# First run over bands: when its statistics, reciprocal roots and biases are issued

## The chip, the cores and the metric

The kernel runs on one core of a Trainium2 chip. The metric is device microseconds of one execution. Engines are called as in the profile: PE (matrix multiply, with PEld for its weight loads), DVE (vector), ACT (scalar functions), POOL (GpSimd) and SP, whose queue issues the transfers. Each engine runs its instructions in the order of its queue.

## The reference

The input x has shape 2 x 256 x 128 x 128 (batch, time, band, channel), float32. Three residual blocks follow one another, each on a layer norm over the 128 channels:

```python
xt = _ln(x, ln_t_w, ln_t_b).transpose(0, 2, 1, 3)
x = x + _mha(xt, t_wi, t_bi, t_wo, t_bo, H_T, cm).transpose(0, 2, 1, 3)
xf = _ln(x, ln_f_w, ln_f_b)
x = x + _mha(xf, f_wi, f_bi, f_wo, f_bo, H_F, bm)
xn = _ln(x, ln_n_w, ln_n_b)
h = jax.nn.gelu(xn @ w1.T + b1, approximate=False)
x = x + (h @ w2.T + b2)
```

The first attention runs over time (256 positions, causal), the second over bands (128 positions, at most 16 apart), both with four heads of 32 channels. The layer norm needs, for each position, the mean, the variance and 1/sqrt(variance + 1e-5).

## The kernel before

**Groups.** The work is cut into 384 groups of 512 positions (four tiles of 128 x 128). Groups 0 to 127 are `OverTime`: the attention over time, whose result goes to a DRAM buffer. After them come 16 runs. Each run has 8 `OverBands` groups and then 8 `FeedForward` groups over the same positions; the result of the bands stays on chip in tiles called x2 (shown as x in the profile). The first run is groups 128 to 135 (bands) and 136 to 143 (feed-forward).

**Steps.** One loop in `BoundedPath.run` goes over n. In step n the engines work on several groups at once: scores and exponentials of group n, the weighing with values and the row sums of group n-1 (`weigh`), their inversion and the division of n-1 (`invert`, `divide`), the output product and residual sum of n-2 (`output`, `finish`), and, for groups ahead, statistics, normalization, a turn through DRAM, and the products for queries, keys and values. Every instruction is pinned to program order (`InOrder`), so the order in which the loop calls these methods is the order of each engine's queue; nothing is moved by the scheduler. PSUM has eight banks that are handed round in turn, or by a fixed table in the time steps; a bank's next use waits for the engine that still reads it.

**Normalizing one group.** `statistics` issues four bn_stats and four bn_aggr on DVE (tiles stats and mv). The root comes in two ways. `root` is done by POOL alone: an addition of epsilon and a power, into rstd. `root_by_scalar` is done by ACT with Ln and Exp (lnv, root), and `refine` follows on DVE with three scalar_tensor_tensor instructions on 128 x 4 elements (vy, vy, rstd). `normalize` issues four tensor_scalar on DVE (xh), `turn` a transpose on DVE (z) and four transfers. Time groups use the second way in step n-5 (statistics and refinement of group n+5 in step n), band and feed-forward groups the first, except those of the first run.

**Biases.** `bias` is one tensor_tensor on POOL per group: x plus a row, into the tile that the group's output is later added to by `finish`. A time step has two masks over 128 x 1024 and two additions on POOL besides the time group's bias; a band step has six masks over 128 x 512 (three of the four heads, two sides). The fourth head's mask is added on DVE (sp<-sp,band). In a feed-forward step of one run POOL also does the bias and the root of the next run's bands.

**The first run.** It has no run before it, so its preparation falls into the last time steps. With A = 8, step n of 120 to 127 issues, after the division, the statistics of group n+8 on DVE and its bias on POOL; step n+1 issues `root_by_scalar` and `refine` of that group. So group 128 has its statistics in step 120 and its refinement in step 121, and group 135 in steps 127 and 128. `normalize` of a band group is in the third step before its own, `finish` in the second after it. Time statistics end with step 122, time normalization with step 123.

Of the kernel before, what the change touches and what calls it, by code (L numbers as in the profile page):

```python
# [25 lines left out]
NT = 4  # L26
GA = 8
GB = 16
RUN = 32
# [698 lines left out]
def time_scores(old, new):  # L728


    if new is not None:
        new.first_tiles()
    if old is not None:
        old.second_tiles()
    for h, second, s in (
        (0, 1, 0), (1, 0, 0), (2, 0, 0), (3, 1, 0), (0, 1, 1), (3, 1, 1), (0, 0, 0), (3, 0, 0),
        (1, 0, 1), (2, 0, 1), (0, 0, 1), (3, 0, 1), (1, 1, 0), (2, 1, 0), (1, 1, 1), (2, 1, 1),
    ):
        if second and old is not None:
            old.second_scores(h, s)  # L740
        if not second and new is not None:
            new.first_scores(h, s)
# [123 lines left out]
class BoundedPath:  # L866
# [164 lines left out]
    def run(self, x, out):  # L1031
        groups = list(self.groups(x, out))

        def do(n, *names):
            if 0 <= n < len(groups):
                for name in names:
                    getattr(groups[n], name)()

        def at(n, kind):
            return 0 <= n < len(groups) and isinstance(groups[n], kind)  # L1040

        def do_at(n, kind, *names):
            if at(n, kind):
                do(n, *names)

        A = RUN // NT

        self.scalar.preload_act_table_set(EXP_SET)
        for n in range(-12, len(groups) + 2):
            feeds = [at(n - 2 + i, FeedForward) for i in range(5)]  # L1050
            bands = [at(n - 2 + i, OverBands) for i in range(5)]
            turn = feeds[2] and bands[1]
            old, new = (groups[i] if at(i, OverTime) else None for i in (n, n + 1))
            self.by_columns = at(n - 1, Attention)
            if bands[2] and feeds[1]:
                self.scalar.preload_act_table_set(EXP_SET)
            do_at(n + 4, FeedForward, "root")
            do(n, "first_half", "first_function", "first_mask")
            if old is not None or new is not None:
                time_scores(old, new)  # L1060
                b = self.banks
                Attention.place = dict(rp=b["b0"], op=b["b3"], yp=b["a1"], qp=b["a2"], kp=b["b1"], vp=b["b2"])
            else:
                Attention.place = {}
            if old is not None:
                old.second_weights(old.late)
            if new is not None:
                new.first_weights(new.early)
            if old is not None:
                old.second_weights(old.early)  # L1070
                old.mask_second()
                old.add(0)
            if turn:
                do(n, "second_half", "second_function")
            do_at(n + 3, OverTime, "fetch")
            do_at(n + 2, (OverBands, FeedForward), "fetch")

            for i in (2 * n + 12, 2 * n + 13) if n < -2 else (n + 10,) if n < 2 else ():
                if i >= NT:
                    do(i, "load")  # L1080
            if n < -8 or n >= 0:
                do(n + 12, "load")
            if n >= 0:
                do_at(n + 5, OverTime, "statistics")
            do_at(n + 3, (OverBands, FeedForward), "normalize", "turn")
            do_at(n + 4, OverTime, "normalize", "turn")
            if n < 0:
                do(n + 5, "statistics")
            do_at(n + 5, FeedForward, "statistics")
            if n == -4:  # L1090
                self.fold_rest()
                self.warm()
            do(n - 1, "weigh")
            do(n - 1, "invert_exactly" if turn else "invert")
            if new is not None:
                new.first_weights(new.late)
                new.mask_first()
            if old is not None:
                old.add(1)
            if bands[2] or turn or old is not None:  # L1100
                do(n - 2, "output", "finish")
            do(n - 1, "divide")
            if not turn:
                do(n, "second_half", "second_function")
            if not bands[2]:
                do_at(n, FeedForward, "bias")
                do_at(n + A, OverBands, "bias")
                if at(n - 1, FeedForward) and at(n - 2, OverBands):
                    do_at(n + A - 1, OverBands, "statistics", "root")
                if not turn:  # L1110
                    do_at(n + A, OverBands, "statistics")
                    if not at(n, OverTime):
                        do_at(n + A, OverBands, "root")
            do_at(n + 2, OverTime, "queries_keys", "take_query", "take_key")
            do_at(n + 1, OverBands, "queries_keys", "take_query", "take_key")
            do_at(n + 5, OverTime, "root_by_scalar", "refine")
            if at(n - 1, OverTime):
                do_at(n + A - 1, OverBands, "root_by_scalar", "refine")
            do_at(n, OverTime, "bias")
            if not bands[2] and not turn and old is None:  # L1120
                do(n - 2, "output", "finish")
            do_at(n + 2, OverTime, "values", "take_values")
            do_at(n + 1, OverBands, "values", "take_values")
            if old is not None or new is not None:

                b = self.banks
                self.banks = dict(
                    a1=b["a1"], a2=b["a2"], b0=b["a0"], b3=b["a3"], a0=b["b0"], a3=b["b1"], b1=b["b3"], b2=b["b2"]
                )
# [69 lines left out]
```

## Time and profile before

| | us |
|---|---|
| median of 4 runs (2729.62 to 2731.49) | 2730.57 |
| the profiled execution's own time | 2729.83 |
| its span in the profile | 2728.1 |
| PE busy | 2698.6 |
| DVE busy | 2282.0 |
| POOL busy | 1864.4 |
| ACT busy | 1847.5 |

The span is the time from the first to the last instruction that the profile holds; the execution's own time has some 1.7 us around it. Busy is the sum of an engine's instructions. A row of the timeline gives start, duration, engine, operation, out<-in, and in brackets the idle time before it and what ended it. In a row of stretches each engine has its busy time and number of instructions, and then come the granted clock of PE (1.00 is full), the share of the DMA engines and what they moved. All instructions issued through the helper have line 861, so they are told apart by their tiles. The time groups end at about 979 us of the span, the first run's band steps at about 1032.

### The profile page before, as it was taken

The page shows a single profiled execution, that of the slowest core. Times are in us where ns is not written, and L with a number is a line of the kernel's source. Part 1 is how long each engine was busy: PE and PEld are TensorE (multiplying, and loading weights), DVE is VectorE, ACT ScalarE, POOL GpSimd, SP SyncE. Part 2 cuts the span into 40 slices and gives each one's busy share as a digit, 9 for nine tenths or more (in the row PEclk, how much of TensorE's full clock was granted, in tenths as well). Part 3 has the DMA queues.
Part 4 walks back from the last instruction along what each step waited for, and adds up shares of the span by engine and source line. Part 5 has one row for each costly group of instructions (what it writes and reads, how often), then busy time and mean ns, then how long its engine had stood idle before and what let it go on. Part 6 is the DMA issues. An engine that isn't in the chain of part 4 may idle for free.

```text
span 2728.1 us, 105787 instructions
## 1 busy us (share of the span) xinstructions
PE 2698.6 (99%) x43538; PEld 1885.2 (69%) x43538; DVE 2282.0 (84%) x6708; ACT 1847.5 (68%) x3620; POOL 1864.4 (68%) x2169
## 2 busy tenths in 40 slices
PE   8999999999999999999999999999999999999998
PEld 5666767767767667676676676766766767767666
DVE  7999999999999997968869779688697796886874
ACT  6888888888888874655745646556556465465563
POOL 3887888888788876666657666666576666665762
PEclk9999999999999999999999999999999999999999
DMA  5555555555555544445444444454453444544533
GB/s 147 145 149 142 146 152 141 148 150 143 143 154 144 135 105 123 114 117 125 112 119 124 108 120 118 117 127 109 120 127 105 120 119 113 133 106 117 133 91 79
DMA packets 471309, 343.83 MB, mean 126 GB/s; under 512 B 43296, under 2 KB 405152, under 8 KB 470816
## 3 DMA queue, kind: packets, MB, share of 16 engines
q1 hardware_dynamic: 469568, 335.92, 48.1%
q8 instruction: 344, 5.64, 0.9%
q14 instruction: 149, 1.22, 0.2%
q10 hardware_dynamic: 1248, 1.05, 0.2%
HBM read 169.03 MB, written 167.77 MB: 123 GB/s over the span
## 4 chain that ended last, share of the span: by engine, by line
PE 73%; DVE 20%; DMA 3%; issue 2%; SPq 1%; POOL 0%; ACT 0%; DVEq 0%; ACTq 0%
PE zp L861 17%; PE hp L861 14%; PE sp L861 8%; PE op L861 6%; PE rp L861 6%; PE vp L861 5%; PE qp L861 5%; PE kp L861 5%; PE yp L861 5%; DVE xh L861 4%; DVE stats L861 3%; DVE u L861 2%; DVE z L861 2%; DVE rp L861 2%; DMA xnT<-turned 2%
## 5 line engine op out<-in xcount | busy, mean ns | idle before, releaser
L861 ACT ACTIVATE hT<-hp,b 128x512 f32<-128x512 f32 x512 | 348.0, 687 | 543.5 <-PE hp L861 532.6
L861 POOL TENSOR_SCALAR_AFFINE_SELECT pf<-pf 128x512 f32<-128x512 f32 x768 | 478.7, 638 | 273.0 <-ACT pf L861 246.8
L861 DVE TENSOR_SCALAR xh<-x,mv,rstd 128x160 f32<-128x160 f32 x1536 | 597.1, 431 | 14.2
L861 PEld LDWEIGHTS zp<-w2T_sb,hT 128*128 128x128 f32 x4096 | 476.3, 192 | 56.2 <-issue 54.1
L861 PE MATMUL zp<-w2T_sb,hT 128*128 128x128 f32 x4096 | 479.8, 275 | 0.1
L861 PE MATMUL hp<-xnT,w1f 128*128 128x512 f32 x1024 | 469.2, 596 | 0.0
L861 ACT ACTIVATE p<-sp 128x512 f32<-128x512 f32 (+1 forms) x1024 | 417.5, 499 | 18.8 <-PE sp L861 6.5
L861 POOL TENSOR_SCALAR_AFFINE_SELECT p<-p 128x1024 f32<-128x1024 f32 x256 | 281.0, 1097 | 185.7 <-ACT p L861 185.6
L861 PE MATMUL sp<-qT,kT 32*128 32x128 f32 (+1 forms) x8192 | 362.9, 310 | 4.7 <-DVE oT L861 2.2
L861 PEld LDWEIGHTS sp<-qT,kT 32*128 32x128 f32 x8192 | 310.6, 185 | 56.0 <-ACT kT L861 44.4
L861 PEld LDWEIGHTS vp<-wf,xnT 128*32 128x32 f32 (+1 forms) x7400 | 237.4, 113 | 153.3 <-issue 137.0
L861 POOL TENSOR_TENSOR p<-p,p 128x512 f32<-128x512 f32 x256 | 329.0, 1285 | 10.7
L861 DVE BATCH_NORM_STATS2 stats<-x 128x6 f32<-128x128 f32 x1536 | 327.0, 275 | 0.1
L861 ACT ACTIVATE pf<-sp 128x512 f32<-128x512 f32 x512 | 264.4, 603 | 58.9 <-PE sp L861 58.7
L861 PEld LDWEIGHTS hp<-xnT,w1f 128*128 128x128 f32 x1024 | 182.1, 190 | 174.7 <-issue 108.9
L861 DVE TENSOR_TENSOR res<-zp,res 128x512 f32<-128x512 f32 x128 | 87.5, 683 | 237.0 <-PE zp L861 237.0
L861 DVE STREAM_TRANSPOSE z<-xh 128x512 f32<-128x512 f32 x384 | 273.3, 712 | 13.2
L861 POOL TENSOR_SCALAR rstd<-mv 128x4 f32<-128x4 f32 x248 | 56.7, 229 | 319.8 <-DVE mv L861 318.9
L861 PE MATMUL vp<-wf,xnT 128*32 128x128 f32 (+1 forms) x7400 | 272.0, 273 | 0.0
L861 PE MATMUL yp<-wn,oT 128*32 128x128 f32 (+1 forms) x7808 | 271.3, 273 | 0.0
L861 POOL TENSOR_TENSOR rstd<-rstd,mhalf 128x4 f32<-128x4 f32 x248 | 256.9, 1036 | 20.7
L861 ACT ACTIVATE qT<-qp,bq 128x512 f32<-128x512 f32 x256 | 176.1, 688 | 138.5 <-PE qp L861 138.5
(92 smaller groups left out, 4217.3 us busy)
## 6 DMA issues: line engine op xcount, KB each, us to landing
turned<-z SPq DMA_DIRECT2D x1536, 64.0 KB, 1.9
xnT<-turned SPq DMA_DIRECT2D x384, 256.0 KB, 3.0
x<-in_x SPq DMA_DIRECT2D x128, 256.0 KB, 4.3
x<-res SPq DMA_DIRECT2D x256, 128.0 KB, 2.4
x<-x SPq DMA_DIRECT2D x128, 256.0 KB, 4.0
out<-res SPq DMA_DIRECT2D x256, 128.0 KB, 2.5
w1T_sb<-in_w1T ACTq DMA_DIRECT2D x1, 256.0 KB, 6.3
w2T_sb<-in_w2T ACTq DMA_DIRECT2D x1, 256.0 KB, 7.7
```

Source lines behind the costliest of these rows:

```text
L861: return self.tc.keep_in_program_order(emit(*args, **kwargs))
```

## The change

The statistics of the eight band groups of the first run no longer follow their place A steps ahead. A table gives each group its step, counted from the first band step 128: group 128 in step 123, 129 and 130 in 124, 131 in 125, 132 in 127, 133 in 128, 134 in 129 and 135 in 130. The statistics are called near the step's start, where those of the time groups are called (after the scores' function and mask of group n, before the normalizations). The root by ACT and the refinement by DVE follow in the same step, in the place after the queries and keys, where those of the time groups are. The biases of these groups are called in their own band steps, 128 to 135, after the division. The other runs keep their order.

```diff
+        run0 = [i for i in range(len(groups)) if at(i, OverBands)][: RUN // NT]
+        due = dict(zip(run0, (-5, -4, -4, -3, -1, 0, 1, 2)))
+        due = {n: [i for i in run0 if run0[0] + due[i] == n] for n in range(-12, len(groups) + 2)}
         A = RUN // NT
...
             if n >= 0:
                 do_at(n + 5, OverTime, "statistics")
+                for i in due[n]:
+                    do(i, "statistics")
...
-            if not bands[2]:
+            if n in run0:
+                do(n, "bias")
+            if not bands[2] and old is None:
                 do_at(n, FeedForward, "bias")
                 do_at(n + A, OverBands, "bias")
                 if at(n - 1, FeedForward) and at(n - 2, OverBands):
                     do_at(n + A - 1, OverBands, "statistics", "root")
                 if not turn:
-                    do_at(n + A, OverBands, "statistics")
-                    if not at(n, OverTime):
-                        do_at(n + A, OverBands, "root")
+                    do_at(n + A, OverBands, "statistics", "root")
...
             do_at(n + 5, OverTime, "root_by_scalar", "refine")
-            if at(n - 1, OverTime):
-                do_at(n + A - 1, OverBands, "root_by_scalar", "refine")
+            for i in due[n]:
+                do(i, "root_by_scalar", "refine")
```

## The prediction

> **What bounds the kernel now.** I read the page's first rows, then busy time by stretches, then the timelines of single engines between 900 and 1040 us. The change touches only steps 120 to 135 of 384, so everything else is a yardstick. A step is named by the loop's n; S(n) is when its scores start on PE: S(120) 914.04, then 921.33, 928.69, 938.15, 946.06, 953.35, 960.64, S(127) 966.41, 978.88, 985.75, 992.79, S(131) 999.23, S(132) 1005.66.
>
> ```profile
> PE 2698.6 (99%) x43538; PEld 1885.2 (69%) x43538; DVE 2282.0 (84%) x6708; ACT 1847.5 (68%) x3620; POOL 1864.4 (68%) x2169
> ```
>
> PE is nearly never idle: what delays PE by a microsecond costs a microsecond. The stretches (span, then busy time of PE, PEld, DVE, ACT, POOL, granted PE clock, DMA) tell where it is delayed:
>
> ```profile
> 914.00:921.30 7.30, 7.30 (x165) 5.07 (x160) 7.09 (x21) 6.45 (x16) 5.91 (x6) 1.00 0.70 184
> 928.70:938.10 9.40, 8.28 (x164) 5.73 (x160) 9.12 (x34) 6.96 (x18) 7.43 (x7) 1.00 0.58 147
> 966.40:969.50 3.10, 0.96 (x12) 0.77 (x9) 2.82 (x7) 1.25 (x5) 3.10 (x4) 0.90 0.34 85
> 969.50:971.00 1.50, 1.48 (x12) 1.15 (x16) 1.47 (x10) 0.25 (x1) 1.50 (x2) 0.50 0.13 22
> 992.80:999.20 6.40, 6.40 (x156) 4.31 (x152) 5.25 (x11) 5.05 (x9) 3.74 (x6) 1.00 0.66 165
> ```
>
> An undisturbed time step takes 7.29 us and a band step 6.43, both with PE full. In a time step DVE is full too (oT to oT 7.27), so it has no room for more. PE's own waits:
>
> ```profile
> 929.77 0.72 PE L861 MATMUL sp<-qT,kT 32*128 32x256 f32 x10 [0.60 <-DVE res L861]
> 931.02 1.44 PE L861 MATMUL sp<-qT,kT 32*128 32x256 f32 x20 [0.53 <-DVE u L861]
> 961.86 1.44 PE L861 MATMUL sp<-qT,kT 32*128 32x256 f32 x20 [0.50 <-DVE u L861]
> 969.52 1.23 PE L861 MATMUL sp<-qT,kT 32*128 32x128 f32 x8 [2.16 <-DVE oT L861]
> 986.40 1.12 PE L861 MATMUL sp<-qT,kT 32*128 32x128 f32 x26 [0.16 <-DVE vy L861]
> 1032.78 1.07 PE L861 MATMUL rp<-pf,ones 128*32 128x512 f32 x8 [0.27 <-DVE u L861]
> ```
>
> Each is a PSUM bank that DVE has not finished with. Step by step, S(n+1)-S(n) exceeds the undisturbed step by 0.07 (step 121), 2.17 (122), 0.62 (123) and 1.06 (126, whose own floor is 4.71, having no queries, keys and values); at 127 PE idles 2.16 us and then runs slowly; at 129 it loses 0.61. On DVE, where the first run's statistics (1.05 to 1.1 us a group) and refinements stand, and on POOL beside it:
>
> ```profile
> 923.20 1.22 DVE L861 SCALAR_TENSOR_TENSOR vy<-mv,root 128x4 f32<-128x4 f32 x1
> 924.46 1.09 DVE L861 SCALAR_TENSOR_TENSOR vy<-vy,root 128x4 f32<-128x4 f32 x1
> 994.18 0.70 DVE L861 TENSOR_TENSOR sp<-sp,band 128x512 f32<-128x512 f32 x1 [1.02 <-PE sp L861]
> 1000.62 0.70 DVE L861 TENSOR_TENSOR sp<-sp,band 128x512 f32<-128x512 f32 x1 [0.84 <-PE sp L861]
> ```
>
> ```profile
> 923.12 1.29 POOL L861 TENSOR_TENSOR res<-x,orow 128x512 f32<-128x512 f32 x1
> 924.44 1.10 POOL L861 TENSOR_SCALAR_AFFINE_SELECT p<-p 128x1024 f32<-128x1024 f32 x1
> 1001.14 3.94 POOL L861 TENSOR_SCALAR_AFFINE_SELECT pf<-pf 128x512 f32<-128x512 f32 x6 [2.50 <-ACT pf L861]
> ```
>
> A vy of four elements takes 0.16 us when POOL is idle, but the two above end with POOL's instruction (923.12+1.29 and 924.44+1.10): refinements wait while POOL works.
>
> **The change, part by part.** Its sum is made against the profiled execution: span 2728.1, its time 2729.83. The median of the runs shown is 2730.57, 0.74 above; I carry the difference over to the median.
>
> *Statistics and refinements leave steps 120 to 122.* The first run's groups 128 to 130 go from steps 120-122, where time statistics are still due, to 123-124, where none are. Steps 121 to 123 return to 7.29: gain 0.07+2.17+0.62 = 2.86.
>
> *Biases leave steps 120 to 127.* One POOL instruction of 1.28 each. A time step has 6.06 us of POOL (two masks 1.10, three tensor_tensors 1.28), with 1.3 idle until ACT's p; with the bias it is 7.3, full, and those masks and biases are what the refinements wait behind. PE itself never waited for POOL there, so the gain is the one above, not another.
>
> *Steps 124 and 125.* Step 124 takes two statistics and two refinements but no normalize and turn (1.58+0.71 less). Its DVE ends 0.5 early (finish 4.96 after S(124), as before, then 2.66 for finish and divide: 7.6, against 8.1 undisturbed). Then the first vy waits for POOL's add (ends 7.86 after S in an undisturbed step), the second for the time bias (9.12), four more take 0.16 to 0.2: 9.9, against 9.44 with one refinement. Delays of DVE come out one to one on PE (oT 2.16 late gave 2.17, 0.61 late gave 0.62). So of the 1.06 at 126, 0.5 stays: between 0 and 1.06, taken at 0.5. Gain 0.56; sum 3.4.
>
> *Step 127's idle stays.* It runs from the first eight scores to oT(125), and oT(125) waits for finish(124), which waits for yp(124) on PE: from yp's start (965.42) to the resume (969.52) 4.10 us, all of PE-to-DVE latency. Statistics taken out of step 126 are not in it (DVE waited 0.21 for that yp). **The clock:** after this gap the granted clock is 0.50 until about 976; rp, op and yp take 1.70, 2.56 and 1.25 us against 0.88, 1.30 and 0.87, the second eight scores some 0.6 more: 3.1 us. [...] The row says that 2.16 us does cool PE here. I take the row: nothing gained, the 3.1 kept as the low end.
>
> *Steps 127 to 131, what is given back.* Groups 133 to 135 now have statistics in DVE's band steps 128 to 130, and refinements 132 to 135 end steps 127 to 130. Counted from oT(126) (979.18 before) that is two more statistics (2.1) and two more refinements (0.44 each): 3.0. Idle there before: 0.85+1.02+0.84 = 2.71. It does not fit neatly, because statistics now follow sp+band and so come after a wait for PE. In coordinates of before: refinement 132 to 979.62, wait for sp(128) to 980.27, then a step of 6.56 us (sp 0.60, stats 1.05, xh 1.64, z 0.63, finish 0.58, rp 0.72, u 0.73, oT 0.61): oT(127) at 986.83 instead of 986.18. The scores of 129 wait for its bank, so PE loses 0.65. Next 987.27, wait to 988.22, 994.78; refinement to 995.22; 1001.78; refinement to 1002.22. Now sp+band of step 131 starts 1.60 late. From there to u(134) at 1032.63 DVE was unbroken before, and PE waited 0.27 for it; so all 1.60 reaches PE at the turn to the feed-forward. After that a few hundred microseconds of PE at 34.00 of 34.00 absorb nothing.
>
> *Biases in steps 128 to 135.* POOL has 3.95 of masks, with 1.28 bias 5.2 of 6.43; from step 132 with the feed-forward roots (0.23+1.04) 6.5. Masks begin 1.92 after S(n) and end 5.85 after it, PE needs them at 7.53: 1.7 of slack hides the 0.1 a step for four steps. Finish of the same group is two steps later. Without that slack it would cost 0.4.
>
> *Roots on ACT* (lnv and root, 0.51): ACT works 5.05 of 6.4 in a band step; what queues behind, the copy of v, is needed by op a step later: nothing. DMAs are the same and keep their places on SP's queue; the x tiles are held up to eight steps longer, but come round only after two further loads: nothing.
>
> [...] Refinement 133 falls at 986.83 (POOL done by 986), 134 at 994.78 (masks from 995.36), 135 at 1001.78, masks from 1001.79. [...] It is nearest to before's 0.44 at 986.18 with POOL free, as POOL's masks start with the scores that DVE itself releases. I take 0 and keep 1.7 for the range, and twice that if 134 is caught too.
>
> **Sum:** -3.4+1.6 = -1.8: 2726.3 of span, 2728.8 of median.
>
> **Rivals.**
> [...]
> - *The band steps hide everything*: the waits are filled, the 1.6 is not lost: 2727.2 (2726.7 with all of the 1.06). For: 2.71 idle. Against: sp+band stands before statistics.
> - *Slower: refinements queue behind masks in steps 129 to 131.* Price 0.65 per instruction behind a mask, up to 1.7 per group, undiminished to the turn. It decides from 1.8 us, so from one group caught wholly and one partly: 2732.2 with both. For: vy 1.22 and 1.09 above. Against: it needs coincidence within 0.6 us.
> - *Nothing moves*: excluded by the order of after's DVE instructions, which stands as written.
>
> **How the numbers follow.** Likeliest 0.47 at 2728.8 (own range 2727.7 to 2730.2: 126's stall from 0 to 1.06, 0.9 of uncertainty in the chain); warm PE 0.23; hidden 0.14; queue behind masks 0.16. The lower end, 2724.2, is warm PE with the 1.6 hidden; the upper, 2732.2, both groups caught. A measurement of this kernel tells about 0.2% from no change, 5.5 us: faster means below 2725.1. That takes warm PE together with half of the 1.6 saved: 0.17. Slower, above 2736.0: locks dearer than any row, 0.06. Within: 0.77.
>
> **What would show it.** Steps 121 to 123 at 7.29; vy short; sp(126) 0.5 late; a wait of 2.2 for oT in step 127, clock 0.50 after it; sp(129) waiting over 1 us; DVE without idle from sp+band(130) on; PE's wait for u at the turn near 1.9 or spread over 132 to 136. Wrong if the clock stays at 1.00, if refinements in band steps take 0.6 and more an instruction, or if oT(127) is not later against S(128).

## The result, and the profile after

The changed kernel takes 2725.61 us (median of 40 runs, 2724.13 to 2729.93) against 2729.40 for the kernel before (60 runs, 2727.02 to 2732.22): ratio 0.9989, 95% interval 0.9984 to 0.9993, or 3.8 us. The forecast was 1.8 us. The profiled execution has 2724.9 us, its span 2723.2 against 2728.1.

Its first row on the page, PE's busy time:

```profile
PE 2694.9 (99%) x43538; PEld 1883.3 (69%) x43538; DVE 2280.5 (84%) x6708; ACT 1846.9 (68%) x3620; POOL 1864.5 (68%) x2169
```

The work is the same to the instruction; PE's busy time is 3.7 us shorter, which already points to a part that ran at another clock. (PE is called cold where its granted clock is 0.50 and warm where it is 1.00.) The stretches of after, with S(121) 920.67, S(126) 957.61, S(127) 962.37, S(128) 971.83 (columns as before: span, busy time of PE, PEld, DVE, ACT, POOL, clock, DMA):

```profile
920.67:928.02 7.35, 7.35 (x164) 5.14 (x160) 7.14 (x21) 6.48 (x16) 6.00 (x6) 1.00 0.53 123
962.37:965.42 3.05, 1.19 (x10) 0.83 (x9) 2.83 (x6) 1.09 (x3) 3.05 (x3) 1.00 0.38 101
965.42:971.83 6.41, 6.41 (x137) 4.21 (x137) 5.40 (x17) 3.29 (x7) 6.18 (x6) 1.00 0.26 74
978.70:986.31 7.61, 7.33 (x156) 4.89 (x152) 6.56 (x22) 5.33 (x12) 4.67 (x8) 1.00 0.26 67
999.18:1006.47 7.29, 6.91 (x156) 4.61 (x152) 7.15 (x24) 5.15 (x9) 6.42 (x10) 1.00 0.49 121
```

The second and third rows are step 127: the gap is there, but the granted clock after it is 1.00, where before had 0.50. The last two are band steps 129 and 132, with 7.61 and 7.29 instead of 7.04 and 6.44. PE's waits in the timeline of after:

```profile
965.42 0.71 PE L861 MATMUL sp<-qT,kT 32*128 32x128 f32 x8 [1.86 <-DVE oT L861]
...
979.92 1.12 PE L861 MATMUL sp<-qT,kT 32*128 32x128 f32 x26 [0.27 <-DVE vy L861]
...
1000.05 1.16 PE L861 MATMUL sp<-qT,kT 32*128 32x128 f32 x28 [0.38 <-DVE x L861]
...
1027.59 1.06 PE L861 MATMUL rp<-pf,ones 128*32 128x512 f32 x8 [0.42 <-DVE u L861]
```

The waits for res and u in steps 122 and 126 are gone. One in step 132 is new, and that at the turn to the feed-forward has grown from 0.27 to 0.42. On DVE, around the refinements and the waits for sp:

```profile
950.59 1.19 DVE L861 SCALAR_TENSOR_TENSOR vy<-vy,root 128x4 f32<-128x4 f32 x1
...
973.15 0.70 DVE L861 TENSOR_TENSOR sp<-sp,band 128x512 f32<-128x512 f32 x1 [0.42 <-PE sp L861]
...
981.09 0.70 DVE L861 TENSOR_TENSOR sp<-sp,band 128x512 f32<-128x512 f32 x1 [0.84 <-PE sp L861]
...
994.83 0.49 DVE L861 SCALAR_TENSOR_TENSOR vy<-vy,root 128x4 f32<-128x4 f32 x1
```

The first ends with POOL's time bias: the wait forecast for step 124. The two waits for sp are where the statistics could have stood. The last waits 0.33 beyond its 0.16, once, behind the first of six masks. POOL beside the first and the last:

```profile
950.49 1.26 POOL L861 TENSOR_TENSOR res<-x,orow 128x512 f32<-128x512 f32 x1
...
994.67 3.95 POOL L861 TENSOR_SCALAR_AFFINE_SELECT pf<-pf 128x512 f32<-128x512 f32 x6 [1.24 <-ACT pf L861]
```

Cut at the same places, from S(121) to the start of rp at the turn, PE's time is (each number a difference of two start times of its timeline; "rest" is steps 128 to the turn):

| kernel | 121-123 | 124-126 | 127 | rest | sum | clock after the gap |
|---|---|---|---|---|---|---|
| before | 24.73 | 20.35 | 12.47 | 53.90 | 111.45 | 0.50 for some 6.8 us |
| after | 21.95 | 19.75 | 9.46 | 55.76 | 106.92 | 1.00 |
| after less before | -2.78 | -0.60 | -3.01 | +1.86 | -4.53 | |
| forecast | -2.86 | -0.56 | 0 | +1.60 | -1.8 | 0.50 |

Spans also differ by some tenths before step 121 (S(121) came 0.66 earlier in after, and lay between 919.4 and 921.3 over all kernels of this study), so the parts are compared by this table and whole kernels by their medians. The times of the changed kernel fall into two groups, 28 of the 40 from 2724.1 to 2726.0 and 12 from 2727.3 to 2729.9, and the upper group has the lower mean granted clock (0.998 in ten of the 12, against 0.999). The profiled execution is of the lower group; of the upper there is no profile.

### The profile page after: what moved, and what is told of

Its sections match the earlier page's. It is cut to its first block, busy times and chain, and to the rows that moved or that the text cites. A ratio compares the mean times of both kernels' runs of the same rounds, so it can differ in the third digit from the quotient of the medians.

```text
span 2723.2 us, 105790 instructions
## 1 busy us (share of the span) xinstructions
PE 2694.9 (99%) x43538; PEld 1883.3 (69%) x43538; DVE 2280.5 (84%) x6708; ACT 1846.9 (68%) x3620; POOL 1864.5 (68%) x2169
## 3 DMA queue, kind: packets, MB, share of 16 engines
q14 instruction: 150, 1.23, 0.2%
q10 hardware_dynamic: 1248, 1.05, 0.2%
## 4 chain that ended last, share of the span: by engine, by line
PE 84%; DVE 12%; DMA 2%; issue 1%; ACT 0%; SPq 0%; DVEq 0%; ACTq 0%
PE zp L861 17%; PE hp L861 14%; PE sp L861 11%; PE op L861 8%; PE rp L861 7%; PE vp L861 7%; PE qp L861 7%; PE kp L861 7%; PE yp L861 6%; DVE xh L861 2%; DVE stats L861 2%; DVE z L861 2%; DVE u L861 2%; DMA xnT<-turned 1%; DVE rp L861 1%; DVE x L861 1%
```

## The experiments

All runs have eleven executions against the kernel before on the same chip. That kernel's median was 2729.21, 2728.70 and 2729.77 on the three chips used, so kernels from different chips are compared by their distance from it. The table after the last of them gives the parts, each from one profiled execution.

**Is it the clock?** Four matmuls without use go into the gap of step 127, in the kernel before and in the changed one:

```diff
+def fill_gap(path, n):
+    bank = path.bank([P, 2 * P], "warm", path.banks["a2"])
+    for _ in range(n):
+        path.tensor.matmul(bank, path.k.ones, path.k.wf[0][:, 0 : 2 * P], start=True, stop=True)
...
+        if new is None and (h, second, s) == (1, 1, 0):
+            fill_gap(old.path, 4)
```

> The kernel before with four extra matmuls (ones by weights, 256 columns, some 0.43 us each, 1.7 us together, result unused) in PE's 2.16 us gap of step 127. Theory C (most of the measured gain is the clock, which the change keeps at 1.00 in step 127 by a gap that is a little shorter or lies elsewhere): granted clock 1.00 from 966 to 976, rp, op and yp at 0.88, 1.30 and 0.87 us, 2.7 to 3.1 us faster than before. Theory S (the gain is the order of the statistics alone, the clock has no part): within 0.5 us of before.

Measured: 2727.01 against 2729.21, ratio 0.9994 (0.9985 to 1.0003); the interval holds no change, so the median alone settles nothing. The profile does: PE of the filled kernel before,

```profile
964.49 1.99 PE L869 MATMUL warm<-wf,ones 128*128 128x256 f32 x8
967.92 0.71 PE L869 MATMUL sp<-qT,kT 32*128 32x128 f32 x8 [1.43 <-DVE oT L869]
968.56 1.07 PE L869 MATMUL rp<-p,ones 128*32 128x256 f32 x16
969.45 1.48 PE L869 MATMUL op<-p,v 128*32 128x256 f32 x32
970.75 1.06 PE L869 MATMUL yp<-wn,oT 128*32 128x128 f32 x32
```

rp, op and yp run at full clock (0.88, 1.30 and 0.87 from start to start), although a wait of 1.43 is left. Steps 126 and 127 together take 15.74 instead of 18.24, the rest is within 0.2 of before. So the slow clock of step 127 is worth 2.67 by the profiles (111.45 and 108.78) and 2.2 by the medians, a little less than theory C gave it.

> The changed kernel with the same four matmuls in its gap. Theory C: PE is warm in every execution, so the times above 2727 that the changed kernel has in some executions are gone and its median falls by 0 to 0.8 us; against the kernel before with the same filling it is 1.3 to 1.8 us faster, which is the order's part alone (3.4 gained, 1.9 given back). Theory S: as the changed kernel, 3.8 us faster than before, with the same spread.

Measured: 2725.08 against 2729.21, ratio 0.9985 (0.9976 to 0.9994), no execution above 2726.63: the upper group is gone. The filled kernels differ by 1.9 us in their medians, and from S(121) to the turn by 1.87 (108.78 and 106.91). That is the order's part with the clock held, close to the 1.8 that the forecast gave to the order alone. The agreement is partly luck: the parts are 2.63 gained in steps 121 to 123, 1.09 in 124 to 127 and 1.85 given back, where 2.86, 0.56 and 1.60 were forecast.

**Which half of the change brings the gain of steps 121 to 126?** First the statistics and roots moved, the biases left in the time steps:

```diff
-            if n in run0:
-                do(n, "bias")
+            if old is not None and n + A in run0:
+                do(n + A, "bias")
```

> The changed kernel with the eight biases left in the time steps 120 to 127, as before. If DVE's excess work in steps 121 to 123 was the cause there, 2.4 to 2.8 us of the 2.8 stay gained, and the give-back after step 128 stays near 1.9, as POOL's biases are no part of it: within 0.7 us of the changed kernel. If refinements waiting behind POOL were the cause, steps 121 to 123 keep stalls of over 1 us and the kernel is 2 us or more slower than the changed one.

Measured: 2729.86 against 2729.21, ratio 1.0004 (0.9995 to 1.0013): no gain at all. (Its profiled execution, 2732.34, is one of its four slowest, so its parts in the table look worse than its median.) DVE in step 121 of this kernel, and POOL at the same time:

```profile
922.07 1.05 DVE L861 SCALAR_TENSOR_TENSOR vy<-mv,root 128x4 f32<-128x4 f32 x1
923.16 1.21 DVE L861 SCALAR_TENSOR_TENSOR vy<-vy,root 128x4 f32<-128x4 f32 x1
924.40 1.09 DVE L861 SCALAR_TENSOR_TENSOR rstd<-vy,root 128x4 f32<-128x4 f32 x1
```

```profile
921.84 1.27 POOL L861 TENSOR_TENSOR x<-x,orow 128x512 f32<-128x512 f32 x1
923.07 1.28 POOL L861 TENSOR_TENSOR res<-x,orow 128x512 f32<-128x512 f32 x1
924.39 1.09 POOL L861 TENSOR_SCALAR_AFFINE_SELECT p<-p 128x1024 f32<-128x1024 f32 x1
```

DVE has no more work here than in any time step, and still its three smallest instructions take 3.35 us, each ending with POOL's instruction beside it; step 122 takes 9.28. Now the biases moved alone, in the kernel before:

```diff
+            if n in range(128, 128 + A):
+                do(n, "bias")
             if not bands[2]:
                 do_at(n, FeedForward, "bias")
-                do_at(n + A, OverBands, "bias")
+                if old is None:
+                    do_at(n + A, OverBands, "bias")
```

> The kernel before with the eight biases alone moved into the band steps 128 to 135; statistics and refinements as before. If DVE's excess work is the cause, steps 121 to 123 still lose 2 us or more and the time is within 1 us of before. If POOL is the cause, the stalls there fall to under 1 us and the kernel is 2 us or more faster.

Measured: 2725.28 against 2729.21, ratio 0.9989 (0.9980 to 0.9998): the gain of the whole change, with the statistics where they were. DVE and then POOL in its step 121:

```profile
920.83 0.86 DVE L861 BATCH_NORM_STATS2 stats<-x 128x6 f32<-128x128 f32 x4
921.60 0.36 DVE L861 BATCH_NORM_AGGREGATE mv<-stats 128x2 f32<-128x6 f32 x4
921.88 0.14 DVE L861 SCALAR_TENSOR_TENSOR vy<-mv,root 128x4 f32<-128x4 f32 x1
922.05 0.16 DVE L861 SCALAR_TENSOR_TENSOR vy<-vy,root 128x4 f32<-128x4 f32 x1
```

```profile
920.61 1.26 POOL L861 TENSOR_TENSOR res<-x,orow 128x512 f32<-128x512 f32 x1
```

The statistics run while POOL does the time bias, until 921.87, and the refinement finds POOL idle. An undisturbed time step has some 0.9 us of such a wait in its first vy (1.05 against 0.14), as DVE and POOL in the kernel before show:

```profile
900.20 1.05 DVE L861 SCALAR_TENSOR_TENSOR vy<-mv,root 128x4 f32<-128x4 f32 x1
```

```profile
899.95 1.27 POOL L861 TENSOR_TENSOR res<-x,orow 128x512 f32<-128x512 f32 x1
```

DVE's own work there is 6.4, not 7.27, and another group's statistics (1.05) and refinement (0.46) make it 7.9: 0.6 over PE's 7.29, not 1.5. Its steps 121, 122 and 123 exceed by 0.04, 0.35 and 0.42, each less than that.

**Does the place of the statistics fill that wait?** As the last kernel, with the statistics behind the refinements:

```diff
-                    do_at(n + A, OverBands, "statistics")
...
             if at(n - 1, OverTime):
                 do_at(n + A - 1, OverBands, "root_by_scalar", "refine")
+            if at(n, OverTime):
+                do_at(n + A, OverBands, "statistics")
```

> As the kernel with the biases alone moved, but in steps 120 to 127 the first run's statistics come after the refinements instead of before them. New account (the time group's refinement waits some 0.9 us for POOL's time bias in an undisturbed step, and statistics put before it fill that wait): the wait returns beside the statistics, steps 121 to 123 lose 1 to 1.5 us each instead of 0.04, 0.35 and 0.42, and the kernel is 2.5 to 3.5 us slower than with the biases alone moved. Old account (DVE is full, so what counts is the amount of work): the same as with the biases alone moved.

Measured: 2727.99 against 2728.70, ratio 0.9995 (0.9986 to 1.0004), 2.7 above the biases alone by the medians, and 3.2 by the distances from the kernel before. Its DVE:

```profile
921.20 1.07 DVE L861 SCALAR_TENSOR_TENSOR vy<-mv,root 128x4 f32<-128x4 f32 x1
...
922.59 0.87 DVE L861 BATCH_NORM_STATS2 stats<-x 128x6 f32<-128x128 f32 x4
...
929.57 0.15 DVE L861 SCALAR_TENSOR_TENSOR vy<-mv,root 128x4 f32<-128x4 f32 x1
```

The wait comes back in the first step, as expected, but only there: 0.9 later, DVE's next refinement finds POOL's bias done, and from then on it takes 7.91 a step (929.57 to 937.48). The steps lose 0.05, 1.08 and 0.62, 0.94 more in sum than with the biases alone, not 1 to 1.5 each. The larger part of the difference is in step 127, 13.07 with a gap of 2.43 and a cold stretch of 6.8 us, against 11.14 with 1.86 and 3.4. So the account of the wait holds, and the price I gave it does not: once the wait had pushed DVE 0.9 later, its next refinements no longer met POOL's bias, while the extra work was paid in every step.

**Do the gains of biases and filling add?** The biases alone moved, with the four matmuls.

```diff
+            if n in range(128, 128 + A):
+                do(n, "bias")
...
+            fill_gap(old.path, 4)
```

> The kernel before with the biases alone moved into the band steps and the four filling matmuls in step 127. If the biases' move takes the stalls of steps 121 to 123 and 126 and the filling keeps the clock at 1.00, as each did alone (4.4 us in the steps, 1.68 of cold clock left in step 127), the two add up to 5.5 to 6.1 us: near 2723.5, 1.5 to 2 us faster than the changed kernel with the filling. If they are the same gain twice, it stays near 2725.

Measured: 2725.32 against 2728.70, ratio 0.9987 (0.9978 to 0.9996). They do not add. The clock is 1.00 and step 127 takes 9.46, 1.68 less, but steps 128 and 129 take 7.27 and 7.72 where the unfilled kernel had 6.87 and 7.04: with PE earlier, DVE is what PE waits for. Two of its refinement's three instructions in step 127 take 0.50 and 1.02 here instead of 0.16, as they take 0.49 and 1.01 in the unfilled kernel, where PE was late enough to hide it; that they wait for POOL once more is my reading, by the sizes alone:

```profile
966.52 0.50 DVE L869 SCALAR_TENSOR_TENSOR vy<-mv,root 128x4 f32<-128x4 f32 x1
...
967.25 1.02 DVE L869 SCALAR_TENSOR_TENSOR rstd<-vy,root 128x4 f32<-128x4 f32 x1
```

PE's wait in step 129:

```profile
980.71 1.12 PE L869 MATMUL sp<-qT,kT 32*128 32x128 f32 x26 [0.27 <-DVE vy L869]
```

Of 1.68, 1.08 is given back.

**What is given back after step 128?** The statistics of groups 133 to 135 of the changed kernel move to the end of the step before:

```diff
         due = dict(zip(run0, (-5, -4, -4, -3, -1, 0, 1, 2)))
+        head = dict(zip(run0, (-5, -4, -4, -3, -1, None, None, None)))
+        tail = dict(zip(run0, (None, None, None, None, None, -1, 0, 1)))
...
-                for i in due[n]:
-                    do(i, "statistics")
+                for i in run0:
+                    if head[i] is not None and run0[0] + head[i] == n:
+                        do(i, "statistics")
...
             for i in due[n]:
                 do(i, "root_by_scalar", "refine")
+            for i in run0:
+                if tail[i] is not None and run0[0] + tail[i] == n:
+                    do(i, "statistics")
```

(The table due still places roots and refinements.)

> The changed kernel with the statistics of groups 133, 134 and 135 at the end of steps 127, 128 and 129, after the refinement, instead of after sp+band in the steps that follow. If the give-back is DVE's wait for PE that the statistics could have filled (0.42 and 0.84 us in the profile of after), oT(127) comes 0.4 to 0.5 earlier, the wait in the scores of 132 shrinks, and the kernel is 0.8 to 1.3 us faster than the changed one. If the give-back is POOL being full in steps 132 to 135, it is within 0.3 us of it.

Measured: 2724.59 against 2729.77, ratio 0.9983 (0.9974 to 0.9992). The rest takes 54.00 instead of 55.76, the whole give-back but 0.1, with the biases still in the band steps and POOL as full as in after. PE's only waits after step 127:

```profile
979.83 1.12 PE L861 MATMUL sp<-qT,kT 32*128 32x128 f32 x26 [0.23 <-DVE vy L861]
1026.24 1.06 PE L861 MATMUL rp<-pf,ones 128*32 128x512 f32 x8 [0.30 <-DVE u L861]
```

So the give-back was DVE waiting for PE in front of work that it could have done, and the biases cost nothing there.

**How long may the gap be?** In the changed kernel the statistics of group 132 go to step 126; and in another, two of the four filling matmuls are used.

```diff
-        due = dict(zip(run0, (-5, -4, -4, -3, -1, 0, 1, 2)))
+        due = dict(zip(run0, (-5, -4, -4, -3, -2, 0, 1, 2)))
```

> The changed kernel with the statistics of group 132 in step 126 instead of 127, which delays oT(125) and makes PE's gap some 0.5 us longer (about 2.4 instead of 1.86). If the length of the gap decides the clock, PE is cold after it in most executions: median 3 us above the changed kernel. [...]

Measured: 2726.80 against 2729.77, ratio 0.9990 (0.9981 to 0.9999), some 1.2 above the changed kernel (0.8 by the distances from the kernel before): more than the 0.40 by which the gap is longer, and short of the 3 expected if its length makes PE cold in most executions. PE's gap and the clock after it:

```profile
965.38 0.71 PE L861 MATMUL sp<-qT,kT 32*128 32x128 f32 x8 [2.26 <-DVE oT L861]
```

```profile
965.50:967.00 1.50, 1.50 (x20) 0.94 (x24) 1.43 (x5) 0.66 (x2) 0.94 (x2) 0.77 0.04 12
967.00:968.50 1.50, 1.50 (x20) 0.77 (x16) 1.43 (x5) 0.67 (x2) 1.42 (x2) 0.50 0.58 163
968.50:970.00 1.50, 1.50 (x32) 1.06 (x28) 0.45 (x1) 0.56 (x1) 1.50 (x2) 0.59 0.09 24
```

PE is cold, but for some 3.4 us instead of 6.8. (In stretches of 0.5 us from 962 to 979 the clock of before is 1.00 or 0.50 but for the two in which it changes, 0.87 and 0.80. Taken so here, the cold time of a row is twice what its clock lacks of 1.00, times its length: 0.69, 1.50 and 1.23.) And it turned cold at about 966.3, when it had been back at work for 0.9 us. Step 127 takes 2.09 more than in after: 0.40 of longer gap and the rest from the clock.

```diff
+            fill_gap(old.path, 2)
```

> The changed kernel with two of the four filling matmuls, 0.86 us, so that some 1 us of the gap stays. If the length of the gap decides, PE is warm in nearly all executions and the time equals that with four. If any gap in the wrong place cools it, a share of executions stays 3 us longer.

Measured: 2725.52 against 2729.77, ratio 0.9986 (0.9977 to 0.9995), no execution above 2726.93; the profile has a gap of 0.74, no cold stretch and step 127 at 9.40. The other ten executions are told only by their times and mean clocks (0.999): they rule out the upper group, but not a cold stretch of 3.4 us, which the kernel with the longer gap has at the same mean clock.

**All together.** Four matmuls, statistics of 132 and 133 in step 127, of 134 and 135 at the end of steps 127 and 128:

```diff
+        head = dict(zip(run0, (-5, -4, -4, -3, -1, -1, None, None)))
+        tail = dict(zip(run0, (None, None, None, None, None, None, -1, 0)))
...
+            fill_gap(old.path, 4)
```

> The changed kernel with four filling matmuls in step 127, the statistics of 133 beside those of 132 in step 127 (DVE waits 0.87 us for yp there), and those of 134 and 135 at the end of steps 127 and 128. If both theories hold, PE warm and give-back gone: 1.3 to 2.1 us faster than the changed kernel with the filling alone, 5.5 to 6.5 us faster than before.

Measured: 2724.43 against 2729.77, ratio 0.9980 (0.9971 to 0.9989), 5.3 us, the lowest of all and just short of the 5.5 expected, and no execution above 2725.39. It is not told apart from the kernel with the statistics earlier (their intervals overlap almost wholly); what the filling seems to add is the absence of late executions (that kernel has two, 2726.83 and 2727.55) and of cold ones (its mean clock is 0.998 in seven of eleven, with the filling in none). PE at the turn waits 0.19, less than before.

The parts of all kernels, cut as above:

| kernel | 121-123 | 124-126 | 127 | rest | sum |
|---|---|---|---|---|---|
| before, filled | 24.57 | 19.36 | 10.95 | 53.90 | 108.78 |
| after, filled | 21.94 | 19.76 | 9.46 | 55.75 | 106.91 |
| after, two matmuls | 21.95 | 19.71 | 9.40 | 55.75 | 106.81 |
| statistics alone | 23.92 | 21.03 | 12.62 | 55.74 | 113.31 |
| biases alone | 22.68 | 19.33 | 11.14 | 53.91 | 107.06 |
| biases alone, statistics last | 23.62 | 19.33 | 13.07 | 53.98 | 110.00 |
| biases alone, filled | 22.70 | 19.36 | 9.46 | 54.99 | 106.51 |
| after, statistics earlier | 21.94 | 19.75 | 9.47 | 54.00 | 105.16 |
| after, longer gap | 21.95 | 19.79 | 11.55 | 55.76 | 109.05 |
| all together | 21.95 | 19.80 | 9.46 | 53.90 | 105.11 |

## Why the prediction was right, and where it was not

The direction was right and the measured 2725.61 lies in the range, but it is 3.8 us faster where 1.8 was forecast.

*"Step 127's idle stays" and "I take the row: nothing gained".* The idle stayed (2.16 became 1.86); the clock did not. This is the term that was mis-sized: 0 forecast, 3.01 gained in the profiled execution; between the medians it is nearer 1.9, the 3.8 less the order's 1.9. The prediction had named a clock that stays at 1.00 as a sign of being wrong here. The row of before showed that a gap had cooled PE, not that it would again. The 40 executions, 28 in the lower group, suggest that most stay warm, or cold for a short time only. The warm PE, to which the prediction gave 0.23, was nearer: with the 3.1 us of the slow clock gained too, its sum is 2725.7. What decides between warm and cold no run shows; 2.16 us was followed by a clock of 0.50 in before, and 1.86 by 1.00 in after and by 0.50 with the biases alone moved.

*"Statistics and refinements leave steps 120 to 122: gain 2.86" and "Biases leave: the gain is the one above, not another".* The size was right (2.78), the owner largely wrong. In steps 121 to 123 moving the statistics alone gains 0.81, moving the biases alone 2.05. Over steps 121 to 126 the statistics alone bring 45.08 to 44.95, the biases alone to 42.01. The sentence "in a time step DVE is full too" failed: 0.9 us of it was a wait for POOL that a busy share counts as work. The rows were there (the 1.22 and 1.09 of the two vy), and I used them for step 124 but not for this step.

*"Steps 124 and 125: 0.5 stays".* 0.37 stayed in step 125, by the very wait named (1.19 in the timeline). Gain 0.60 against 0.56.

*"What is given back".* 1.60 forecast, 1.86 measured: 0.57 at the scores of 129 (0.65 forecast), 0.85 in step 132, the rest, 0.44, in the steps to the turn. The kernel with the statistics earlier shows the cause to be the one given, statistics behind a wait for PE.

*Refinements behind masks.* The rival "refinements queue behind masks" cost 0.33 once (a vy of 0.49 instead of 0.16), far from the 1.8 from which it would have decided. No run shows the 1.7 that the upper end of the range counts for each group caught; that 0.33 was measured in its place. In the time steps a refinement's wait for POOL was worth more than I gave it: vy took 1.05, 1.22 and 1.09 instead of 0.14 to 0.16, each ending with POOL's instruction, and that is what the biases' move gains.

*Biases in band steps, roots on ACT.* Nothing, as forecast: POOL is full in steps 133 to 135 (masks without idle before them), and yet with the biases alone moved, steps 128 to the turn take 53.91, as before (53.90).

## What to carry to other kernels

A busy engine may be waiting inside its instructions: a tiny instruction that takes several times its usual time, and ends with another engine's (here vy, 1.22 instead of 0.16), is a wait, and its owner is found by moving that other engine's work alone. When a change moves two things at once, run each alone before giving one of them the gain. And where PE idles for around 2 us, as here (2.16 with a clock of 0.50 after it, 1.86 with 1.00 or 0.50), take the clock as a case with its own time, not as a constant: one profile shows one outcome.

## What the runs showed of the hardware

- PE's clock after a gap: in the profiles, gaps of 2.16 (before and with the statistics alone), 2.26 and 2.43 us were followed by a cold stretch; of three profiles with 1.86, two stayed warm and one (biases alone) turned cold; 0.74, and 1.43 behind the filling matmuls, stayed warm.
- The cold stretch lasted 3.4 us (biases alone, longer gap) or 6.8 (before, statistics alone, statistics last). It began 1.5 to 3.6 us after the gap's start: in the three long cases while PE still idled, in the two short ones 0.9 and 1.8 us after it was back at work at 1.00. So no single delay from the gap's start fits these five profiles. What decides at 1.86 is left open, as no run here shifts the gap by itself.
- The refinements' scalar_tensor_tensor (vy and rstd, 0.13 to 0.17 with POOL idle) ended in several places together with an instruction of POOL: at 1.22 and 1.05 with a tensor_tensor of 1.28, at 1.09 with an affine_select of 1.10, and once at 0.49 with the first of six masks of 0.64. bn_stats ran beside a tensor_tensor and beside an affine_select at its usual 0.86 for four. With the biases alone moved, steps 121 to 123 took 22.68 with statistics in front of the refinement and 23.62 with statistics behind it.

The rows that show the shorter cold stretch, with the biases alone moved: PE is back at 965.11, the clock falls at about 966.9 and is 1.00 again at about 970.3.

```profile
965.11 0.71 PE L861 MATMUL sp<-qT,kT 32*128 32x128 f32 x8 [1.86 <-DVE oT L861]
```

```profile
965.50:967.00 1.50, 1.50 (x30) 0.95 (x31) 1.43 (x9) 0.77 (x3) 1.34 (x2) 0.96 0.22 63
967.00:968.50 1.50, 1.50 (x24) 0.90 (x19) 1.50 (x4) 1.12 (x2) 1.42 (x2) 0.50 0.29 112
968.50:970.00 1.50, 1.50 (x32) 1.47 (x28) 1.36 (x3) 0.00 (x0) 1.50 (x2) 0.50 0.00 0
970.00:971.50 1.50, 1.50 (x32) 0.88 (x26) 0.69 (x2) 0.00 (x0) 1.48 (x2) 0.90 0.22 52
```
